# The matrices loaded behind one 512 KB load instead of two, and a slot of input released ahead of VectorE's copies

## The chip, the cores and the metric

One core of a Trainium2 chip. The metric is the device time of one execution in microseconds; lower is better. A core has TensorE (PE: matrix products, from SBUF into PSUM), VectorE (DVE), ScalarE (ACT), GpSimd (POOL) and SyncE (SP), each with an instruction stream of its own, and sixteen DMA engines between HBM and SBUF. The engines order their work by semaphores.

## The reference

```python
# x: (128, 128, 1024) f32; subjects: (128,) int32 in 0..7; weights: (8, 128, 128) f32
w = weights[subjects]
out = jnp.einsum('bct,bcd->bdt', x, w)
return x + out
```

For each of 128 batch entries a 128 x 128 matrix is chosen out of eight by an index, its transpose is multiplied with the entry's 128 x 1024 block, and the block is added. 67 MB are read and 67 MB written.

## The kernel before

The residual is taken into the product: the identity is added to the chosen matrix, so that one product gives x + out. VectorE builds these matrices at run time from the index: `place_rows` (lines 207 to 216) adds `eye` to `w_nat`, the matrices as loaded, and `place` (195 to 205) adds `same` to `w_all`, the matrices in another order of rows.

The batch is worked in 32 tiles of four entries (2 MB in, 2 MB out each). `x_in` has four slots, `x_out` eight. The two sets of PSUM banks, `ps[0]` and `ps[1]`, hold two entries each.

The first four tiles are loaded entry by entry (`load_rows`, 163 to 170: 512 KB each, so sixteen loads), with one row of the entry to a partition; all four slots are filled at the start without any wait. The matrices (512 KB, in rows of 512 B) come between the second and the third of these loads (lines 300 to 307). Sorting matmuls (355 to 363) then bring the matrices into the row order of the later tiles, in `ps[1]`; ACT and VectorE each copy half of that into `w_all` (`sort`). The later 28 tiles are loaded in two transfers of 1 MB (`load`, 151 to 161).

All loads are issued by ACT, all stores by SP, each in program order. A slot of `x_in` may be filled anew when its tile has been multiplied. VectorE says so with `s_eaten`, and ACT waits for it ahead of each load (lines 368 and 374). In the long loop ACT first does its own copies of a tile (`take`), then waits for `s_eaten`, then issues the two loads of the tile four places on.

VectorE's work for one tile: wait for a free output slot (`s_room`), wait for a product (`s_product`), copy it from PSUM to `x_out`, twice, then build the matrices of the tile two places on with four small products (`place_rows` or `place`). `signal` (416 to 419) hangs the tile's signals on these products: the first tells SP that the copies are done (`s_added`), the second releases the input slot (`s_eaten`), the last tells TensorE that the matrices are there (`s_go`). In the first four tiles VectorE makes both copies (`copy_rows`, whole bank sets); in the later ones it copies `ps[0]` in two halves, and ACT copies `ps[1]` with a swap of partition halves.

TensorE multiplies a tile when its matrices (`s_go`) and its input (`s_ready`, passed on by POOL from the loads' semaphores) are there and the banks are free (`s_free`). POOL waits in order for stores (`s_out`, which gives `s_room`) and loads (`s_in`, which gives `s_ready`).

Of the kernel before, what the change touches and what calls it, by code (L numbers as in the profile page):

```python
# [30 lines left out]
H = 2  # L31

P = 2
# [18 lines left out]
FIRST = 4  # L52
# [5 lines left out]
def transfer(nc, engine, out, in_):  # L58

    later, nc._always_lower_symbolic_ap = nc._always_lower_symbolic_ap, False
    ins, outs = engine.lower_ap_dma(in_), engine.lower_ap_dma(out)
    nc._always_lower_symbolic_ap = later
    return engine.add_instruction(
        mybir.InstDMACopy(
            name=nc.get_next_instruction_name(),
            engine=engine.engine,
            ins=ins,
            outs=outs,  # L70
            mode="Copy",
            cce_op=ALU.bypass,
            queue=QUEUES[engine.engine],
        )
    )
# [3 lines left out]
def kernel(  # L79
# [7 lines left out]
    nc = tc.nc  # L87
# [3 lines left out]
    Q = P * H  # L91
# [12 lines left out]
    if room:  # L104
# [26 lines left out]
    s_eye = tc.alloc_semaphore("s_eye")  # L131
# [4 lines left out]
    s_eaten = tc.alloc_semaphore("s_eaten")  # L136
    s_product, s_added, s_free, s_room = (
        [tc.alloc_semaphore(f"s_{name}{p}") for p in range(P)]
        for name in ("product", "added", "free", "room")
    )  # L140
# [22 lines left out]
    def load_rows(i, q):  # L163
        at = (i % IN * Q + q) * T
        transfer(
            nc,
            nc.scalar,
            x_in[:, at : at + T],
            x[i * Q + q].rearrange("(b r) t -> b (r t)", r=C // 32),
        ).then_inc(s_in[i % IN], DMA)  # L170
# [14 lines left out]
    def subjects_of(at):  # L185
        _, subject = nc.values_load_multi_w_load_instructions(
            index[0:1, at],
            engines=[mybir.EngineType.DVE],
            min_val=0,
            max_val=S - 1,  # L190
            skip_runtime_bounds_check_because="the index is clamped on the chip above",
        )
        return subject

    def place(u, subject):
        return [
            nc.vector.tensor_tensor(  # L197
                ws[u][p][h * A : (h + 1) * A],
                w_all[h * A : (h + 1) * A, bass.ds(subject[p * H + h], 1), :],
                same[h * A : (h + 1) * A],  # L200
                ALU.add,
            )
            for p in range(P)
            for h in range(H)
        ]

    def place_rows(u, subject):
        return [
            nc.vector.tensor_tensor(  # L209
                ws[u][q // H][:, :, q % H * D : (q % H + 1) * D],  # L210
                w_nat[:, bass.ds(subject[q], 1), :],
                eye,
                ALU.add,
            )
            for q in range(Q)
        ]
# [42 lines left out]
    def half_of(slot, half):  # L259
        at = slot * (P * SIZE) + half * T  # L260
        banks = slice(half * (T // N), (half + 1) * (T // N))
        return at, banks

    def copy(slot, half):
        at, banks = half_of(slot, half)
        return nc.vector.tensor_copy(  # L266
            x_out[:, bass.ds(at, T)], ps[0][:, banks].rearrange("d b n -> d (b n)")
        )

    def copy_rows(i, p):  # L270
        at = i % OUT * P * SIZE + p * SIZE
        return nc.vector.tensor_copy(  # L272
            x_out[:, at : at + SIZE], ps[p].rearrange("d b n -> d (b n)")
        )
# [22 lines left out]

    with tc.tile_critical():  # L298

        for q in range(H):  # L300
            load_rows(0, q)
        transfer(
            nc,
            nc.scalar,
# [42 lines left out]
        for p in range(P):  # L347
            nc.gpsimd.wait_ge(s_same, H).then_inc(s_room[p], OUT - p * FIRST)

        for q in range(H, FIRST * Q):  # L350
            load_rows(q // Q, q % Q)

        nc.tensor.wait_ge(s_pick, 1)
# [51 lines left out]
        placed = place_rows(0, subject[:Q])  # L405
# [5 lines left out]
        placed = place_rows(1, subject[Q:])  # L411
# [3 lines left out]

        def signal(placed):
            placed[0].then_inc(s_added[0], 1)
            placed[1].then_inc(s_eaten, 1)
            placed[-1].then_inc(s_go, 1)

        for i in range(FIRST):
            subject = subjects_of(slice((i + 2) * Q, (i + 3) * Q))
            nc.vector.wait_ge(s_room[0], 1).then_inc(s_room[0], -1)
            for p in range(P):
                nc.vector.wait_ge(s_product[p], 1).then_inc(s_product[p], -1)  # L425
                copy_rows(i, p).then_inc(s_free[p], 1 if i < FIRST - 1 else R * (1 + p))
            signal((place_rows if i + 2 < FIRST else place)(i % 2, subject))
        with nc.vector.Fori(0, (NT - FIRST) // 2) as turn:  # L428
            for u in range(2):
                subject = subjects_of(bass.ds(turn * (2 * Q) + (u + FIRST + 2) * Q, Q))  # L430
                slot = (turn * 2 + (u + FIRST)) % OUT
                nc.vector.wait_ge(s_room[0], 1).then_inc(s_room[0], -1)
                for half in range(2):
                    nc.vector.wait_ge(s_product[0], H).then_inc(s_product[0], -H)  # L434
                    copied = copy(slot, half).then_inc(s_free[0], 1)
                signal(place(u, subject))
        with nc.tensor.Fori(0, FIRST // 2) as turn:
            for u in range(2):
# [44 lines left out]
```

## Time and profile before

| | before |
|---|---|
| median of 3 runs, us | 328.47 (328.0 to 329.03) |
| profiled execution: its own time, us | 328.55 |
| profiled execution: span, us | 326.8 |
| PE / DVE / ACT / POOL busy | 77% / 44% / 37% / 1% |
| HBM read and written, MB | 67.63 and 67.11 |
| mean over the span, GB/s | 412 |

The span runs from the first to the last event of one execution as the hardware profiler saw it. A page of the profile gives busy time by engine, the span in 40 slices of 8.17 us, queues, and groups of instructions. ACTq and SPq are the instructions with which ACT and SP issue transfers; the transfers run later, on the DMA engines. "L65 DMA_DIRECT2D" is the line of the helper `transfer` that every load and store goes through. In a timeline, a row has its start, its length (of all instructions merged into it), engine, line, operation, output and input; in brackets stands the idle time ahead of it and what ended it. The rows on which the prediction rests stand there.

### The profile page before, as it was taken

How to read it: one execution, taken by the hardware profiler on the slowest of the kernel's cores; microseconds unless marked ns; L12 is line 12 of the kernel's file. 1: busy time of each engine (PE TensorE's matmuls, PEld its weight loads, DVE VectorE, ACT ScalarE, POOL GpSimd, SP SyncE). 2: the span in 40 equal slices, each digit the busy share in tenths (PEclk: the TensorE clock that was granted, in tenths of full speed). 3: DMA queues.
4: the chain of work that ended last, by engine and by line, in shares of the span. 5: the costliest groups of instructions: out<-in, count | busy, mean ns of one | idle time of the engine just before them, and what ended most of it. 6: DMA issues, size and time to landing. Idle time of an engine off the chain costs nothing. (4 is left out here: it accounts for less than half of the span.)

```text
span 326.8 us, 5288 instructions
## 1 busy us (share of the span) xinstructions
PE 251.4 (77%) x1870; PEld 93.5 (29%) x1870; DVE 143.4 (44%) x207; ACT 120.3 (37%) x142; POOL 1.8 (1%) x8
## 2 busy tenths in 40 slices
PE   6899968888888888887495886958886827999300
PEld 2344423333333333333131332313332302333100
DVE  1377855555555555555504455044555050555500
ACT  0200005555555555555504555045555050555500
POOL 2000000000000000000000000000000000000000
PEclk9799999999999999999978999789999776999955
DMA  6999999999999999999999999999999999999990
GB/s 238 424 415 311 434 423 433 428 419 441 423 435 429 429 431 427 435 427 429 427 439 427 419 450 441 425 417 415 453 419 439 437 413 429 449 429 409 441 445 40
DMA packets 8247, 134.81 MB, mean 413 GB/s; under 512 B 1585, under 2 KB 2610, under 8 KB 2610
## 3 DMA queue, kind: packets, MB, share of 16 engines
q10 hardware_dynamic: 4496, 67.64, 49.1%
q1 hardware_dynamic: 3746, 67.11, 48.3%
q8 instruction: 2, 0.03, 0.0%
q14 instruction: 3, 0.02, 0.0%
HBM read 67.63 MB, written 67.11 MB: 412 GB/s over the span
## 5 line engine op out<-in xcount | busy, mean ns | idle before, releaser
L249 PE MATMUL ps<-x_in,w 64*64 64x512 f32 x1792 | 213.5, 619 | 49.6 <-PEq L240 47.5
L278 ACT COPY x_out<-ps 64x1024 f32 (+1 forms) x112 | 112.6, 1006 | 173.5 <-ACTq L293 167.5
L266 DVE COPY x_out<-ps 128x1024 f32 x56 | 68.6, 1224 | 143.6 <-DVEq L434 143.6
L249 PEld LDWEIGHTS ps<-x_in,w 64*64 64x64 f32 x1792 | 77.5, 138 | 185.5 <-issue 185.5
L197 DVE TENSOR_TENSOR w<-w_all,same 64x256 f32<-64x256 f32 x120 | 50.4, 420 | 3.2
L225 PE MATMUL ps<-x_in,w 128*128 x64 | 27.6, 592 | 0.0
L272 DVE COPY x_out<-ps 128x2048 f32<-128x2048 f32 x8 | 18.3, 2291 | 6.0 <-DVEq L425 6.0
L225 PEld LDWEIGHTS ps<-x_in,w 128*128 128x128 f32 x64 | 12.2, 190 | 15.3 <-issue 15.3
L357 PE MATMUL ps<-x_out 128*128 128x512 f32 x8 | 5.4, 836 | 2.3 <-DMA x_out<-in_L_cond_weights_dram 2.3
L313 PE MATMUL ps<-x_out 128*128 128x512 f32 x6 | 5.1, 1028 | 1.7 <-DVE x_out L310 1.7
L209 DVE TENSOR_TENSOR w<-x_out 128x128 f32<-128x128 f32 x16 | 3.6, 285 | 6.1 <-DMA x_out<-in_L_cond_weights_dram 5.9
L284 ACT ACT_TABLE_LOAD x1 | 1.3, 1283 | 12.9 <-issue 12.9
L296 ACT COPY mark<-same 1x1 f32 (+1 forms) x28 | 5.3, 190 | 0.7
L357 PEld LDWEIGHTS ps<-x_out 128*128 128x128 f32 x8 | 2.0, 263 | 6.0 <-issue 6.0
L284 DVE COPY w_all<-ps 128x1024 f32<-128x1024 f32 x1 | 1.2, 1225 | 4.4 <-PE ps L357 4.4
L313 PEld LDWEIGHTS ps<-x_out 128*128 128x128 f32 x6 | 1.8, 328 | 3.7 <-issue 2.1
L284 ACT COPY w_all<-ps 128x1024 f32<-128x1024 f32 x1 | 1.0, 1012 | 0.3 <-PE ps L357 0.3
L310 DVE MEMSET x_out<- 128x512 f32 x1 | 0.5, 485 | 1.0 <-SPq L298 1.0
L381 DVE TENSOR_SCALAR x_out<-x_out 1x128 int32<-1x128 int32 x1 | 0.4, 395 | 0.6 <-DMA x_out<-in_itok_B_dram 0.6
L338 POOL TENSOR_SCALAR_AFFINE_SELECT same<-same 128x256 f32<-128x256 f32 x1 | 0.5, 526 | 0.1
L326 POOL TENSOR_SCALAR_AFFINE_SELECT x_out<-x_out 128x256 f32<-128x256 f32 x1 | 0.4, 423 | 0.0
L338 POOL TENSOR_SCALAR_AFFINE_SELECT same<-x_out 128x256 f32<-128x256 f32 x1 | 0.4, 417 | 0.0
(9 smaller groups left out, 1.4 us busy)
## 6 DMA issues: line engine op xcount, KB each, us to landing
x_in<-in_x_dram ACTq DMA_DIRECT2D x56, 1024.0 KB, 14.3
out_dram<-x_out SPq DMA_DIRECT2D x20, 2048.0 KB, 57.3
out_dram<-x_out SPq DMA_DIRECT2D x6, 4096.0 KB, 45.7
x_in<-in_x_dram ACTq DMA_DIRECT2D x16, 512.0 KB, 9.4
x_out<-in_L_cond_weights_dram ACTq DMA_DIRECT2D x1, 512.0 KB, 6.8
x_out<-in_itok_B_dram SPq DMA_DIRECT2D x1, 0.5 KB
```

Source lines behind the costliest of these rows:

```text
L197: nc.vector.tensor_tensor(ws[u][p][h * A : (h + 1) * A], w_all[h * A : (h + 1) * A, bass.ds(subject[p * H + h], 1), :], same[h * A : (h + ...
L209: nc.vector.tensor_tensor(ws[u][q // H][:, :, q % H * D : (q % H + 1) * D], w_nat[:, bass.ds(subject[q], 1), :], eye, ALU.add,)
L225: mm = nc.tensor.matmul(ps[p][:, bank], ws[u][p][:, 0, h * D : (h + 1) * D], x_in[:, bass.ds(slot * (Q * T) + ((p * H + h) * T + t), N)], ...
L249: mm = nc.tensor.matmul(ps[p][cols, bank], ws[i % 2][p][rows, 0, r * D + e * A : r * D + (e + 1) * A], x_in[rows, at : at + N], start=r == ...
L266: return nc.vector.tensor_copy(x_out[:, bass.ds(at, T)], ps[0][:, banks].rearrange("d b n -> d (b n)"))
L272: return nc.vector.tensor_copy(x_out[:, at : at + SIZE], ps[p].rearrange("d b n -> d (b n)"))
L278: return nc.scalar.copy(x_out[h * A : (h + 1) * A, bass.ds(at + SIZE, T)], ps[1][(1 - h) * A : (2 - h) * A, banks].rearrange("d b n -> d ( ...
L284: engine(w_all.rearrange("c s (r e a) -> c r s e a", r=R, e=R)[:, r], ps[1][:, r * R : (r + 1) * R].rearrange("c g (s a e) -> c (g s) e a" ...
L296: nc.scalar.copy(mark[:, bass.ds(slot, 1)], same[:1, 0, :1]).then_inc(s_added[1], 1)
L313: nc.tensor.matmul(ps[P - 1][:, BANKS - 1], zeros[:, :D], zeros, start=True, stop=True)
L338: nc.gpsimd.affine_select(same[:, 0, :], same[:, 0, :] if h else zeros[:, : R * D], [[2 * C, R], [-2 * C, R], [-1, A]], ALU.not_equal, 1.0 ...
L357: nc.tensor.matmul(ps[1][:, r * R + g], pick[:, r], w_raw[:, g * N : (g + 1) * N], start=True, stop=True,).then_inc(s_picked, 1)
```

## The change

The matrices are issued behind one load of 512 KB instead of two; the second load of tile 0 moves behind them, the order of the rest stays. And the signal `s_eaten` leaves `signal`: VectorE gives it by an instruction of its own, which stands right behind its wait for the tile's last product and ahead of the copy of that product. The instruction waits for `s_eye`, a semaphore that was set at the start and is never taken back, so that it does not hold anything up.

```diff
-        for q in range(H):
-            load_rows(0, q)
+        load_rows(0, 0)
         transfer(
             nc,
             nc.scalar,
...
-        for q in range(H, FIRST * Q):
+        for q in range(1, FIRST * Q):
             load_rows(q // Q, q % Q)
...
         def signal(placed):
             placed[0].then_inc(s_added[0], 1)
-            placed[1].then_inc(s_eaten, 1)
             placed[-1].then_inc(s_go, 1)
+
+        def eaten():
+            nc.vector.wait_ge(s_eye, 1).then_inc(s_eaten, 1)
...
                 nc.vector.wait_ge(s_product[p], 1).then_inc(s_product[p], -1)
+                if p == P - 1:
+                    eaten()
                 copy_rows(i, p).then_inc(s_free[p], 1 if i < FIRST - 1 else R * (1 + p))
...
                     nc.vector.wait_ge(s_product[0], H).then_inc(s_product[0], -H)
-                    copied = copy(slot, half).then_inc(s_free[0], 1)
+                    if half:
+                        eaten()
+                    copy(slot, half).then_inc(s_free[0], 1)
```

On ACT, at the very start of the program, the order of the transfers changes (`in_L_cond_weights_dram` is the matrices, `in_x_dram` the input; a line number is that of the kernel concerned, and moves by what is added or taken above it):

```order
-L479 UNCONDITIONAL_BRANCH x2
-L65 DMA x_in<-in_x_dram 128x1024 x2
+L484 UNCONDITIONAL_BRANCH x2
+L65 DMA x_in<-in_x_dram 128x1024
 L65 DMA x_out<-in_L_cond_weights_dram 128x8x128
-L65 DMA x_in<-in_x_dram 128x1024 x14
+L65 DMA x_in<-in_x_dram 128x1024 x15
 L284 ACT_TABLE_LOAD
 L284 COPY w_all<-ps 128x8x128
```

The matrices stand second instead of third; the sixteen loads stay sixteen.

On VectorE, in each of the first four tiles, with the semaphores that a row waits for (those of the semaphore instructions ahead of it are shown with it):

```order
 L186 TENSOR_LOAD index [waits s_same]
 L272 COPY x_out<-ps 128x2048 [waits s_room0,s_product0]
-L272 COPY x_out<-ps 128x2048 [waits s_product1]
+L272 COPY x_out<-ps 128x2048 [waits s_product1,s_eye]
 L209 ISA
 L209 TENSOR_TENSOR w<-x_out 128x128
```

The release stands between the wait for `s_product1` and the second copy; before, it hung on the second of the products that follow in the last row.

## The prediction, made before the changed kernel was run

> **What bounds the kernel now.** I read the page's slices first, then the stretches of the transfers, then the start instruction by instruction.
>
> ```profile
> PE 251.4 (77%) x1870; PEld 93.5 (29%) x1870; DVE 143.4 (44%) x207; ACT 120.3 (37%) x142; POOL 1.8 (1%) x8
> DMA  6999999999999999999999999999999999999990
> GB/s 238 424 415 311 434 423 433 428 419 441 423 435 429 429 431 427 435 427 429 427 439 427 419 450 441 425 417 415 453 419 439 437 413 429 449 429 409 441 445 40
> HBM read 67.63 MB, written 67.11 MB: 412 GB/s over the span
> ```
>
> No engine is full; the DMA row is, in every slice but the first and the last. The rate stays near 430 GB/s except in slice 0 (238), slice 3 (311, the time from 24.5 to 32.7 us) and the last. So the kernel is bound by the bytes: 134.74 MB at 430 GB/s are 313.3 us, and what a change can win lies in the places where the transfers run below 430. The stretches around them (busy time of each engine, then granted clock, DMA share and GB/s):
>
> ```profile
> 0.00:2.00 2.00, 0.33 (x1) 0.33 (x2) 0.51 (x3) 0.00 (x0) 0.36 (x5) 1.00 0.00 0
> 2.00:5.00 3.00, 3.00 (x4) 1.18 (x4) 1.01 (x3) 0.00 (x0) 1.42 (x4) 1.00 0.98 339
> 5.00:9.00 4.00, 1.80 (x3) 0.34 (x1) 0.00 (x0) 0.00 (x0) 0.00 (x0) 1.00 0.88 307
> 9.00:24.00 15.00, 14.90 (x31) 6.59 (x32) 7.83 (x13) 2.29 (x2) 0.00 (x0) 0.89 1.02 431
> 24.00:26.00 2.00, 2.00 (x6) 0.86 (x5) 1.66 (x4) 0.00 (x0) 0.00 (x0) 1.00 0.74 311
> 26.00:33.00 7.00, 7.00 (x18) 3.12 (x17) 5.52 (x7) 0.00 (x0) 0.00 (x0) 1.00 0.99 309
> 33.00:60.00 27.00, 23.36 (x149) 9.05 (x147) 16.57 (x19) 5.77 (x7) 0.00 (x0) 1.00 1.01 429
> 60.00:309.00 249.00, 199.04 (x1664) 72.05 (x1664) 110.26 (x161) 112.21 (x134) 0.00 (x0) 0.95 1.01 431
> 321.10:325.30 4.20, 0.00 (x0) 0.00 (x0) 0.00 (x0) 0.00 (x0) 0.00 (x0) 0.50 0.05 23
> ```
>
> Against 430 GB/s the stretches lose: 2 to 5 us, 3 x (1 - 339/430) = 0.63 us; 5 to 9 us, 4 x (1 - 307/430) = 1.14; 24 to 26 us, 2 x (1 - 311/430) = 0.55; 26 to 33 us, 7 x (1 - 309/430) = 1.97. With 2 us before the first byte, 2.0 + 0.63 + 1.14 + 0.55 + 1.97 + 313.3 = 319.6 us. The span is 326.8: in the last 7 us the share is 0.05 of sixteen engines, so a single late engine sets the end.
>
> The two losses at 24 to 33 us are of different kinds: at 24 to 26 the share is 0.74, engines stand idle; at 26 to 33 the share is 0.99 and the rate 309, they are busy but slow. Why they stand idle, by the timeline of ACT (the loads' queue), SP (the stores') and VectorE:
>
> ```profile
> 0.91 1.18 ACTq L65 DMA_DIRECT2D x_in<-in_x_dram  x2
> 2.12 0.66 ACTq L65 DMA_DIRECT2D x_out<-in_L_cond_weights_dram  x1
> 2.81 10.05 ACTq L65 DMA_DIRECT2D x_in<-in_x_dram  x14
> 12.90 1.28 ACT L284 ACT_TABLE_LOAD   x1 [12.90 <-issue]
> 14.51 1.01 ACT L284 COPY w_all<-ps 128x1024 f32<-128x1024 f32 x1 [0.33 <-PE ps L357]
> 24.29 1.26 ACTq L65 DMA_DIRECT2D x_in<-in_x_dram  x2
> ...
> 24.00 21.39 SPq L65 DMA_DIRECT2D out_dram<-x_out  x4
> ...
> 9.19 0.90 DVE L209 TENSOR_TENSOR w<-x_out 128x128 f32<-128x128 f32 x4 [5.91 <-DMA x_out<-in_L_cond_weights_dram]
> 15.89 0.90 DVE L209 TENSOR_TENSOR w<-x_out 128x128 f32<-128x128 f32 x4 [0.15 <-DVE w_all L284]
> 18.06 2.29 DVE L272 COPY x_out<-ps 128x2048 f32<-128x2048 f32 x1 [1.28 <-DVEq L425]
> 21.48 2.29 DVE L272 COPY x_out<-ps 128x2048 f32<-128x2048 f32 x1 [1.13 <-DVEq L425]
> 23.69 0.89 DVE L209 TENSOR_TENSOR w<-x_out 128x128 f32<-128x128 f32 x4
> ```
>
> Sixteen loads and the matrices, 17 x 0.524 = 8.91 MB, are queued at the start. Up to 24.0 us the stretches moved 1.02 + 1.23 + 6.47 = 8.7 MB, so the queue runs dry at about 24.5. The next load is issued only at 24.29, behind VectorE's two copies and two products of tile 0 (23.69 + 2 x 0.22 = 24.1), and the first store at 24.00. Both need over a microsecond before bytes move (the first load: issued 0.91, no byte before 2), hence the hole.
>
> **The change: the earlier matrices.** They are issued second instead of third: 1.49 instead of 2.12 (half of 1.18 us earlier, 0.6), behind 0.524 MB less, which at 339 GB/s is 1.55 us. So they land between 0.6 and 1.55 us earlier than now; I take 1.2, and TensorE's first use of them moves from 9.10 to about 7.9.
>
> ```profile
> 9.10 5.37 PE L357 MATMUL ps<-x_out 128*128 128x512 f32 x8 [2.30 <-DMA x_out<-in_L_cond_weights_dram]
> 14.30 27.63 PE L225 MATMUL ps<-x_in,w 128*128 x64
> ...
> 11.00:12.00 1.00, 1.00 (x2) 0.34 (x1) 0.00 (x0) 0.00 (x0) 0.00 (x0) 0.50 0.88 377
> ```
>
> The eight sorting matmuls take 5.37 us now, part of it at a granted clock of 0.50; at full clock one takes 27.63 / 64 = 0.43, eight 3.45. They end between 11.4 and 13.3 instead of 14.30; tile 0's five transfers, 2.62 MB, are in by about 10 as now (2.25 MB up to 9.0, the rest at 431 GB/s). That is not all kept: half of tile 0's products wait for the PSUM banks of the sort, which go free after ACT's copy, and ACT stands in its issues until 12.86, then 1.28 of table load and 1.01 of copy: 15.2 against 15.5 now. So tile 0's second half starts between 15.8 (VectorE's first product behind that copy) and 16.8 (13.3 + 3.45), and ends 3.45 later, 19.3 to 20.2, against 14.30 + 16 x 0.43 = 21.2. VectorE's copy of it and the first store move by the same 1 to 1.9 us: the store to about 22.5.
>
> **The earlier release.** It goes from the second product at 24.1 to the moment when VectorE sees tile 0's second half, 21.5 now and 19.8 with the earlier matrices. ACT waits for nothing else there, so the load of tile 4 is issued near 20, some 4.3 us earlier, while 4.5 us of the first loads still lie in the queue. It cannot land sooner for that, but the queue no longer runs dry: the hole at 24 to 26 goes, 0.55 us.
>
> In the long loop the release gains nothing. There ACT itself is last:
>
> ```profile
> 140.14 4.10 ACT L278 COPY x_out<-ps 64x1024 f32 x4 [3.84 <-ACTq L293]
> 144.23 0.48 ACTq L65 DMA_DIRECT2D x_in<-in_x_dram  x1
> ...
> 143.18 1.76 DVE L197 TENSOR_TENSOR w<-w_all,same 64x256 f32<-64x256 f32 x4
> ```
>
> VectorE's second product ends at 143.18 + 0.88 = 144.06, ACT's own copies, ahead of the load on its queue, at 144.24. The new instruction on VectorE waits for a semaphore long set. One such step shows in the chain as
>
> ```profile
> 305.24 0.06 DVEq L266
> ```
>
> so 32 of them cost 1.9 us of an engine that is 44% busy; behind each stands only the second copy, and TensorE's next tile needs ACT's four copies of 4.10 us anyway, so nothing. Without that cover it would be 28 x 0.06 = 1.7 us. What stands behind on SP and POOL are waits for VectorE's and the loads' signals, which come earlier.
>
> **The slow stretch, 26 to 33 us.** No row shows it without the hole ahead of it. From below: if it comes from starting both queues anew after the hole, it goes with it, a gain of 1.97. From above: if it comes from the loads meeting the first stores, it only moves, 0. Nearest row: 33 to 60 us, where stores of the same four first tiles meet loads at 429 GB/s, so the meeting alone does not cost. I take three quarters, 1.5 us.
>
> The Trainium skill, "DMA: Bandwidth & Descriptors", section "Latency and other measured facts", gives 207 GB/s for copies whose rows lie 512 KiB apart. The first four stores write rows of 4 KB whose four heads are 512 KB apart; by that rule the stretch is the stores' own and would stay (the second rival). The row of 33 to 60 us speaks against it as a whole, the one of 26 to 33 for it where stores run nearly alone.
>
> **The opening, 2 to 9 us.** The same 17 transfers in another order. The matrices' small rows keep costing what they cost (1.14 at 5 to 9); I take 0. At best all of that goes, -1.14; at worst the engines are done with the first load 1.55 us earlier while the matrices are issued only 0.6 earlier, and wait 0.9.
>
> **Sum.** -0.55 - 1.5 + 0 = -2.05 against the profiled execution's 328.55, which is 0.08 above the median of 328.47: 326.5.
>
> **Rivals.** *The late engine keeps the end.* One engine still moves bytes from 321.1 to 325.3 us when the others are done. An engine that is behind has no hole at 24 to 26 (it is still on its first loads when the others stop), so it may gain nothing from the filled hole, and the others' gain ends in a longer wait for it. For it: the share of 0.05. Against: the slow stretch has share 0.99, so it costs that engine too. *The stretch stays.* By the pitch of the first stores only the hole goes: 328.55 - 0.55 = 328.0. Both give 327.6 to 329.0, no change.
>
> *Slower: the matrices are drawn before they are ready.* In 5 to 9 us the share is already 0.88. If the engines stand for the matrices' 1024 small rows behind one load, each loses up to 0.9 us, the late one too; with nothing back at 24 to 33 that is 328.55 + 0.9 = 329.5. It decides from a share below about 0.7 in 4 to 8 us. Against it: issue to first byte was about 1.4 us for the first load, and 1.49 + 1.4 = 2.9 is ahead of that load's end.
>
> *The change does nothing to the loads*: a load issued 4 us earlier waits 4 us longer. Then only holes are worth anything, which is how the sum is made; it belongs to the 328.0 above.
>
> **How the numbers follow.** A gain or loss under 0.3% (1 us) cannot be told from no change here. Forecast, a gain of 1 to 3.7 us: 0.60, most likely 326.5. Late engine or lasting stretch, within 0.3%: 0.29. Slower by over 0.3%: 0.11. The low end: 328.55 - 0.55 - 1.97 - 1.14 = 324.9. The high end takes in the no-change rivals and part of the slower one: 329.2.
>
> **What would show it.** Matrices: the sorting matmuls begin at 7.5 to 8.5 instead of 9.10. Release: a load issue at 19.5 to 20.5 instead of 24.29, a store issue near 22.5. Hole: 24 to 26 us at about 430 GB/s instead of 311. Stretch: 26 to 33 us above 400. Opening: 2 to 9 us no lower than (3 x 339 + 4 x 307) / 7 = 321 GB/s. It is wrong if 24 to 33 us reads 430 and the time stands (late engine), if the low rates return later (stretch), or if the opening falls under 300 (matrices).

## The result and the profile after

| | before | after |
|---|---|---|
| median, us | 328.00 (326.53 to 329.26, 17 runs) | 326.43 (325.62 to 328.88, 17 runs) |
| ratio | | 0.9957, 95% interval 0.9940 to 0.9973 |
| profiled execution / its span, us | 328.55 / 326.8 | 328.88 / 327.1 |

The change makes the kernel 0.43% faster, 1.4 us (0.9 to 2.0). The profiled execution of after happens to be the slowest of its 17 runs; a second profile of the same kernel, 326.80 us with a span of 325.0, stands beside it below (experiment e4). The page of after, the two rows of the transfers in 40 slices:

```profile
DMA  7999999999999999999999999999999999999890
GB/s 230 423 429 427 422 441 423 426 437 419 435 439 421 437 435 425 425 445 421 431 421 439 425 420 435 429 431 459 419 425 431 433 417 425 421 437 437 385 393 20
```

Slice 3, 311 GB/s before, is now 427. In return slices 37 and 38, near the end, have fallen to 385 and 393. The stretches of after (granted clock, DMA share and GB/s at a row's end):

```profile
2.00:5.00 3.00, 3.00 (x4) 1.18 (x4) 1.00 (x3) 0.00 (x0) 1.43 (x4) 1.00 0.86 263
5.00:9.00 4.00, 3.71 (x8) 1.39 (x7) 0.90 (x4) 0.00 (x0) 0.00 (x0) 1.00 1.01 356
9.00:24.00 15.00, 14.00 (x33) 5.91 (x32) 9.11 (x12) 2.29 (x2) 0.00 (x0) 1.00 1.01 428
24.00:26.00 2.00, 2.00 (x6) 0.81 (x5) 0.75 (x2) 0.00 (x0) 0.00 (x0) 1.00 1.02 418
26.00:33.00 7.00, 7.00 (x18) 3.17 (x17) 5.33 (x6) 0.00 (x0) 0.00 (x0) 1.00 0.98 419
321.10:325.30 4.20, 0.00 (x0) 0.00 (x0) 0.00 (x0) 0.00 (x0) 0.00 (x0) 0.50 0.05 23
```

The hole at 24 to 26 us is closed (share 1.02 instead of 0.74), and the slow stretch behind it is gone too (419 GB/s instead of 309). The last row has not changed: one engine of sixteen is still at work when the others are done. The start of after, from the timelines of ACT, SP, VectorE and TensorE:

```profile
1.49 0.66 ACTq L65 DMA_DIRECT2D x_out<-in_L_cond_weights_dram  x1
12.08 1.28 ACT L284 ACT_TABLE_LOAD   x1 [12.08 <-issue]
13.38 1.01 ACT L284 COPY w_all<-ps 128x1024 f32<-128x1024 f32 x1
19.10 8.01 ACTq L65 DMA_DIRECT2D x_in<-in_x_dram  x4
...
21.60 32.99 SPq L65 DMA_DIRECT2D out_dram<-x_out  x5
...
14.54 0.90 DVE L209 TENSOR_TENSOR w<-x_out 128x128 f32<-128x128 f32 x4 [2.75 <-ACT w_all L284]
19.08 2.29 DVE L272 COPY x_out<-ps 128x2048 f32<-128x2048 f32 x1 [1.15 <-DVEq L426]
...
6.86 3.67 PE L356 MATMUL ps<-x_out 128*128 128x512 f32 x8 [0.29 <-DMA x_out<-in_L_cond_weights_dram]
11.53 27.99 PE L225 MATMUL ps<-x_in,w 128*128 x64 [1.00 <-PEq L222]
```

The sorting matmuls start at 6.86 instead of 9.10 and take 3.67 instead of 5.37. The load of tile 4 is issued at 19.10, the moment when VectorE starts its second copy (19.08), instead of 24.29; the first store goes at 21.60 instead of 24.00.

### The profile page after: what moved, and what is told of

Its sections match the earlier page's. It is cut to its first block, busy times and chain, and to the rows that moved or that the text cites. A ratio compares the mean times of both kernels' runs of the same rounds, so it can differ in the third digit from the quotient of the medians.

```text
span 327.1 us, 5320 instructions
## 1 busy us (share of the span) xinstructions
PE 250.2 (76%) x1870; PEld 93.7 (29%) x1870; DVE 143.4 (44%) x207; ACT 120.4 (37%) x142; POOL 1.8 (1%) x8
## 2 busy tenths in 40 slices
DMA packets 8247, 134.81 MB, mean 412 GB/s; under 512 B 1585, under 2 KB 2610, under 8 KB 2610
## 5 line engine op out<-in xcount | busy, mean ns | idle before, releaser
L249 PEld LDWEIGHTS ps<-x_in,w 64*64 64x64 f32 x1792 | 78.5, 138 | 186.2 <-issue 186.2
L312 PE MATMUL ps<-x_out 128*128 128x512 f32 x6 | 4.9, 982 | 1.7 <-DVE x_out L309 1.7
L356 PE MATMUL ps<-x_out 128*128 128x512 f32 x8 | 3.7, 601 | 0.3 <-DMA x_out<-in_L_cond_weights_dram 0.3
```

The lines of the kernel that those rows point to most:

```text
L249: mm = nc.tensor.matmul(ps[p][cols, bank], ws[i % 2][p][rows, 0, r * D + e * A : r * D + (e + 1) * A], x_in[rows, at : at + N], start=r == ...
L312: nc.tensor.matmul(ps[P - 1][:, BANKS - 1], zeros[:, :D], zeros, start=True, stop=True)
L356: nc.tensor.matmul(ps[1][:, r * R + g], pick[:, r], w_raw[:, g * N : (g + 1) * N], start=True, stop=True,).then_inc(s_picked, 1)
```

## The experiments

All are compared with the kernel before, run on the same chip beside them. Between the sets of runs the median of the kernel before differs by up to 0.7 us (327.69 to 328.36), so medians of different sets are compared only roughly. The theory: the rates at 24 to 33 us were lost because the queues ran dry. Its rivals: the slow stretch belongs to the first stores, or a late DMA engine sets the end.

**e1: the matrices alone.**

```diff
-        for q in range(H):
-            load_rows(0, q)
+        load_rows(0, 0)
...
-        for q in range(H, FIRST * Q):
+        for q in range(1, FIRST * Q):
```

> Only the matrices move ahead of the second load; the release stays on the second product. Theory (the hole is what costs; whatever brings the load of tile 4 well ahead of 24.5 us, when the first loads end, wins all of it): VectorE's second product of tile 0 comes at 21.7 us (21.29 + 2 x 0.22 in the changed kernel), the load of tile 4 is issued at about 21.9, and 24 to 33 us read 415 to 430 GB/s as with both parts; ratio to before 0.995 to 0.997. Rival (the two gains add up, each part half): the stretch 24 to 33 us stays between 309 and 419 GB/s and the ratio is 0.997 to 0.999.

**e2: the release alone** (`eaten()` as in the change, the matrices third as before).

> Only the release moves ahead of the copies; the matrices stay third. Theory of the hole: the load of tile 4 is issued at 21.5 us (VectorE's second copy began at 21.48 before), three microseconds ahead of the end of the first loads, and 24 to 33 us read 415 to 430 GB/s though stores still start at 24.0; ratio 0.995 to 0.997. Rival (gains add up): 309 to 419 GB/s, ratio 0.997 to 0.999.

The first load issued after the start, and the stretch of 24 to 33 us, of e1, then of e2:

```profile
21.71 8.05 ACTq L65 DMA_DIRECT2D x_in<-in_x_dram  x4
24.00:33.00 9.00, 9.00 (x22) 3.99 (x21) 6.38 (x8) 0.00 (x0) 0.00 (x0) 1.00 1.02 431
```

```profile
21.25 8.01 ACTq L65 DMA_DIRECT2D x_in<-in_x_dram  x4
24.00:33.00 9.00, 9.00 (x22) 3.98 (x22) 7.29 (x9) 0.00 (x0) 0.00 (x0) 1.00 1.02 417
```

Each part by itself issues the load three microseconds ahead of the end of the first loads, and each brings the rate of 24 to 33 us back (431 and 417, before 309; in e2 the part from 26 to 33 us alone reads 393). By the rates the parts do not add up. The ratios are 0.9978 (0.9951 to 1.0006) and 0.9977 (0.9952 to 1.0002). Both lie in the range that the rival had named, and both intervals reach 1: by the times alone, each part can be told neither from no change nor from both together.

**e3: the first four stores in the later stores' layout**, in the kernel before.

```diff
-        if i < FIRST:
+        if i < 0:
             there = out[i * Q : (i + n) * Q].rearrange("g d t -> d g t")
```

> The kernel before, with one change: the first four stores write rows of 8 KB with heads 1 MB apart, as the later ones do, so that the first four tiles land in another order in the output than the reference's. Theory of the hole: the slow stretch stays, 26 to 33 us at 290 to 340 GB/s, time as before (ratio 0.998 to 1.002). Rival (the stretch belongs to the 4 KB rows 512 KB apart): 26 to 33 us read over 400 GB/s, only the hole at 24 to 26 stays, ratio 0.993 to 0.996.

Its sorting matmuls, the next load, and the two stretches:

```profile
9.02 6.53 PE L357 MATMUL ps<-x_out 128*128 128x512 f32 x8 [3.10 <-DMA x_out<-in_L_cond_weights_dram]
25.37 1.26 ACTq L65 DMA_DIRECT2D x_in<-in_x_dram  x2
24.00:26.00 2.00, 2.00 (x6) 0.92 (x5) 1.66 (x6) 0.00 (x0) 0.00 (x0) 1.00 0.26 107
26.00:33.00 7.00, 7.00 (x18) 3.06 (x17) 5.52 (x7) 0.00 (x0) 0.00 (x0) 1.00 1.05 337
```

Stores in a layout that runs at 431 GB/s later on are followed by the same slow stretch, 337 GB/s. And in after, e1 and e2 the first stores keep their rows, and the stretch is gone. So it is not the rows of the first stores; it follows the hole. The hole itself came out larger (107 GB/s), because the sort took 6.53 us instead of 5.37 at the low clock (below) and the load went 1.1 us later. Ratio 1.0025 (0.9995 to 1.0056).

**e4: both parts again**, the changed kernel, for a second profile.

> The changed kernel once more, for a second profile. Theory of the late engine: its last bytes land some 5 to 6 us behind the fifteen others (at 319 us) in this profile too, and the profiled execution's time follows it. Rival (that late engine belonged to one execution): the last engine is done within 3 us of the others and the profiled execution takes about 326.4 us. Ratio to before 0.995 to 0.997 by both.

The end of the kernel before, of after, and of e4 as the transfers show it between 316 and 327 us, in 40 slices of 0.275 us:

```profile
DMA  9022920299022800200020000200020000000000
```

```profile
DMA  0982299820000200020002000020002000000000
```

```profile
DMA  0209520292000020002000020000000000000000
```

A 2 that stands alone is one packet: a single engine takes one every 1.2 us when the fifteen others are done. From 319.6, 318.2 and 318.5 us on they come singly, and the last one starts at 324.0, 324.3 and 322.3 us. So the late engine is there each time, about 4 to 6 us behind, and the time of the execution follows it: 328.55, 328.88 and 326.80 us. The ratio of e4 is 0.9969 (0.9944 to 0.9994).

Ahead of the last store, by the stretch up to it, of before and of e4, each with the issue of that store:

```profile
307.00:309.50 2.50, 0.00 (x0) 0.00 (x0) 1.28 (x4) 0.71 (x2) 0.00 (x0) 1.00 0.98 419
308.65 0.54 SPq L65 DMA_DIRECT2D out_dram<-x_out  x1
```

```profile
307.00:309.00 2.00, 0.00 (x0) 0.00 (x0) 1.19 (x3) 0.48 (x2) 0.00 (x0) 0.51 0.20 82
308.50 0.54 SPq L65 DMA_DIRECT2D out_dram<-x_out  x1
```

Here most of the gain of the fifteen went. Before, they were busy until the last store (0.98). In e4 the share from 307 to 309 us is 0.20: they have run out of work and stand idle, 2 x (1 - 0.20) = 1.6 us, for a last store that is issued only 0.15 us earlier.

**e6: POOL lets TensorE start ahead of its wait for the output slot.**

```diff
+            landed = DMA * (Q + P * (i // IN))
+            nc.gpsimd.wait_ge(s_in[i % IN], landed).then_inc(s_ready, 1)
             if i - OUT in stored:
                 n, count = stored[i - OUT]
                 for p in range(P):
                     nc.gpsimd.wait_ge(s_out[i % OUT], count).then_inc(s_room[p], n)
-            landed = DMA * (Q + P * (i // IN))
-            nc.gpsimd.wait_ge(s_in[i % IN], landed).then_inc(s_ready, 1)
```

> The changed kernel, with POOL's two waits for a tile in the other order: the loads' (which lets TensorE start) ahead of the stores' (which frees the output slot). Now tile 28's products wait until 271 us for a store that the late engine finishes at 269.6. Theory (the late engine sets the end by its own work): tile 28 is multiplied some 7 us sooner, the last store is issued earlier, the fifteen engines are done earlier, and the end stays: ratio to before 0.994 to 0.998 as with the change alone. Rival (the end follows the last store, which follows the last four tiles): the end moves by 3 us or more with the last store, ratio 0.984 to 0.989.

Tile 28 on TensorE and the last store, in e4 and in e6, and the transfers of e6 between 316 and 327 us:

```profile
271.00 9.71 PE L249 MATMUL ps<-x_in,w 64*64 64x512 f32 x64 [7.29 <-PEq L240]
...
308.50 0.54 SPq L65 DMA_DIRECT2D out_dram<-x_out  x1
```

```profile
260.36 7.45 PE L249 MATMUL ps<-x_in,w 64*64 64x512 f32 x64 [2.65 <-PEq L240]
...
304.69 0.54 SPq L65 DMA_DIRECT2D out_dram<-x_out  x1
...
DMA  9890222020002000020002000000000000000000
```

Tile 28 is multiplied 10.6 us sooner, and the last store goes 3.8 us sooner. The last single packet starts at 321.8 us, only 0.5 us sooner than in e4, and the time hardly moves: median 326.09 against 326.43 and 326.48 of the changed kernel. The ratio is 0.9926 (0.9895 to 0.9958); e7, which is compared with the same runs of the kernel before, has 0.9932. The last store does not set the end; the rival (at most 0.989) is out. It is the lowest median of the study, but it cannot be told from the changed kernel.

**e7: the matrices ahead of all loads.**

> The changed kernel, with the matrices ahead of all loads instead of behind one. Theory (earlier matrices are worth only the hole, and that is closed): the sorting matmuls start about 1.2 us earlier than in the changed kernel if TensorE is free (it is busy with its idle products until 6.6, so at 6.6), 24 to 33 us stay at 415 to 430 GB/s, ratio to before 0.994 to 0.998, the same as with the change. Rival (the start of the chain itself is worth time): another 0.5 to 1.2 us, ratio 0.991 to 0.994.

The sorting matmuls:

```profile
6.95 3.65 PE L355 MATMUL ps<-x_out 128*128 128x512 f32 x8
```

They start at 6.95 us as in e4, without an idle time ahead of them: until then TensorE is at its idle products. The median, 326.47, is that of the change (326.43 and 326.48). The ratio, 0.9932 (0.9901 to 0.9964), lies in the rival's range, and its interval covers the theory's too; e6, which starts as the change does, has 0.9926 against the same runs. So no gain on the change is seen, but a small one is not excluded. The rate of 24 to 33 us is 408 GB/s, a little under what was expected.

**e5: the last store over fifteen engines.**

```diff
-    def store(i, n):
+    def store(i, n, rows=slice(None)):
...
-            there,
-            x_out[:, at : at + n * P * SIZE].rearrange("a (o f) -> a o f", o=1),
+            there[rows],
+            x_out[rows, at : at + n * P * SIZE].rearrange("a (o f) -> a o f", o=1),
...
-    last = store(*stores[-1])
...
+    for rows in (slice(0, 120), slice(120, C)):
+        last = store(*stores[-1], rows)
...
```

> The changed kernel, with the last store (4 MB) cut in two: 120 partitions, which the transfer can only spread over fifteen DMA engines, and the 8 others. One engine, if it is the last of the sixteen, so has up to 9.75 us less to move (319.6 - 309.9 in the kernel before, from its start to the end of the fifteen), the others 0.65 us more (9.75 x 128/120), eight of them a row of 1.2 us besides. Theory (one engine that is behind sets the end, and it is always this one): the end falls to that of the others, 320.5 to 321.5 us, ratio to before 0.984 to 0.990. Rival a (it is another engine, or one that changes): the end is 0.6 to 1.9 us later than with the change, ratio 0.998 to 1.003. Rival b (the late engine is only what the profile shows, not what bounds the timed runs): ratio within 0.998 to 1.003 too, with the tail gone in the profile.

```profile
309.00:320.00 11.00, 0.00 (x0) 0.00 (x0) 0.00 (x0) 0.00 (x0) 0.00 (x0) 0.50 0.90 241
```

A miss: ratio 1.0207 (1.0127 to 1.0287). In this row of its stretches the engines are busy (0.90) and move 241 GB/s, where e4 has 384. This store of 120 partitions is slow in itself, so the run tells nothing about the late engine.

**e8 to e11: extra work for some of the engines.**

```diff
+            if i == NT - 4:
+                nc.sync.wait_ge(s_spare, 8 * DMA)
             store(i, n).then_inc(s_out[i % OUT], DMA)
+            if i == 8:
+                there = out.rearrange("b (a r) t -> (b a) (r t)", r=R)[(NT - 1) * Q * A :]
+                for j in range(8):
+                    rows = slice(j * 8, (j + 1) * 8)
+                    transfer(
+                        nc, nc.sync, there[rows], w_all[rows].rearrange("c s d -> c (s d)")
+                    ).then_inc(s_spare, DMA)
```

> The changed kernel, with eight extra stores of 8 partitions each behind the ninth store (8 rows of 8 KB from w_all, into rows of the last tile that are written over later). A transfer of 8 rows can be spread over eight DMA engines at most, so eight engines have 64 KB more each, 2 x 1.22 = 2.4 us. Theory (one engine, always the same, is 4 to 6 us behind and sets the end; the others have that much in hand): the end moves by 2.4 us if that engine is among the eight (ratio to before about 1.003), and by nothing if it is not (about 0.996, as with the change alone). Rival (all engines bound the time, through the stores that every tile waits for): 8/16 of it, 1.2 us, ratio 0.9995.

> The same with 12 rows in each extra store, twelve engines at most. Theory: 2.4 us if the late engine is among the twelve (ratio about 1.003), nothing if not (0.996). Rival: 12/16 of it, 1.8 us, ratio 1.001.

> The same with 15 rows, fifteen engines at most. Theory: 2.4 us unless the late engine is the one left out (ratio 1.003, or 0.996). Rival: 15/16 of it, 2.3 us, ratio 1.003.

> The same with 16 rows, all sixteen engines: 1 MB more in all, 2.4 us. Both: the end moves by 2.4 us against the change alone, ratio to before about 1.003. If it does not, the extra work lies in time in which the late engine stands idle, and the reading of the other three falls.

The packets of the kernel before and of e8:

```profile
DMA packets 8247, 134.81 MB, mean 413 GB/s; under 512 B 1585, under 2 KB 2610, under 8 KB 2610
DMA packets 8375, 135.33 MB, mean 414 GB/s; under 512 B 1649, under 2 KB 2674, under 8 KB 2674
```

The eight extra stores bring 128 packets: 64 of 8 KB with the rows, and 64 under 512 B (1649 instead of 1585), eight for each store, which fits a store that is cut in eight parts.

| rows in an extra store | median, us | ratio to before | over the change's 326.45 |
|---|---|---|---|
| 8 | 328.98 | 1.0045 (1.0012 to 1.0079) | 2.5 |
| 12 | 329.11 | 1.0035 (1.0010 to 1.0059) | 2.7 |
| 15 | 329.14 | 1.0053 (1.0027 to 1.0079) | 2.7 |
| 16 | 329.97 | 1.0078 (1.0051 to 1.0105) | 3.5 |

The last column compares different sets of runs; from the ratios and the change's 0.9957 it would be 2.9, 2.6, 3.1 and 4.0 us. Either way, half of the engines with 2.4 us more already cost the whole 2.4 us; a share of 1.2 us would have been 0.9995, outside the interval. That does not yet single out one engine: any engine held up by 2.4 us might cost as much. That the sixteenth engine costs another 0.8 us was not foreseen and stays open.

**e12: stairs.** The same place, with two stores each of 1, 2, ... 8 rows.

> The changed kernel, with the extra stores as stairs: two each of 1, 2, ... 8 rows of 8 KB. A store of k rows goes to the first k engines, so the first engine gets sixteen rows more (16 x 0.31 = 4.9 us), the next fourteen, and so on to the eighth with two (0.6 us). Theory (one engine among the first eight is 4 to 6 us behind; the others have that much in hand): the end moves by that engine's own extra alone, 0.6 us for the eighth, 1.2 for the seventh, up to 4.9 for the first: ratio to before 0.998 for the eighth, 1.001 for the sixth, 1.007 for the third, 1.011 for the first. Anything well under 4.9 us shows that engines with more extra work than that had it in hand. Rival (any engine that is held up by so much sets the end): 4.9 us, ratio 1.011.

Median 329.11, ratio 1.0021 (0.9998 to 1.0044), 2.7 us more than the change (2.1 by the ratios). If the rows fall on the engines as expected, an engine with 4.9 us of extra work does not delay the end by 4.9 us, so engines are there that have time in hand, and that rival (1.011) is out. By the stairs and the interval the late engine would be about the fourth to the seventh, but e11 shows that the extra stores cost something besides, so which one it is stays open. No row of the profile numbers the engines. That a transfer of k rows goes to the lowest-numbered k engines is what the Trainium skill states ("DMA: Bandwidth & Descriptors", section "Why a DMA increments its semaphore by 16 and not by 1"); the sizes of the effects do not speak against it, and nothing here shows it directly. So the stairs argue for one late engine; they do not show it.

## Why the prediction was right, and where its size was off

**The earlier matrices:** the first use came at 6.86 instead of 7.5 to 8.5, 2.2 us earlier than before and so beyond the bound of 1.55 us that the prediction gave; why is not shown. The sort then ran at full clock and was over at 10.5. Tile 0's second half waited for ACT's copy, as said, but ACT's issues ended at 12.06 and not at 12.86 as in the kernel before, so the copy began at 13.38, VectorE's products behind it at 14.54 instead of 15.8, and the second half was seen at 19.08 instead of 19.3 to 20.2. All of this only feeds the hole, as said; e7 shows no gain from more of it.

**The release:** right, with the load at 19.10 (said 19.5 to 20.5) and the store at 21.60 (said 22.5), each a little earlier, as the second half was. That it gains nothing in the long loop was not tried by itself; the rate of 60 to 309 us, 431 GB/s before and 430 in e2, shows no gain there.

**The hole, 0.55 us, and the slow stretch, 1.5 of 1.97 us:** both went, the stretch more than the three quarters taken: at 24 to 33 us after and e4 read 419 and 430 GB/s against 309, which is 9 x 110 / 430 = 2.3 us and 2.5 us. e1 and e2 show that either way to an early load does it; e1, e2 and e3 refute the rival of the first stores' rows. In these stores only the four heads of one partition lie 512 KB apart; the rows of neighbouring partitions lie 4 KB apart. Nor do stores run nearly alone in the stretch, as the prediction read it: 1.11 MB of stores and 1.05 MB of loads start in it. Why the engines run slow for 7 us after a hole is not shown; the trace shows that each packet takes longer (a 16 KB packet of the stores 0.80 us on average, in the next 7 us 0.61; a 32 KB packet of the loads 1.77, then 1.21).

**The opening, 0:** (3 x 263 + 4 x 356) / 7 = 316 GB/s against 321, 0.1 us lost. Right.

**The sum, 2.05 us:** measured 1.4, interval 0.9 to 2.0. By the rates the regained time was, if anything, larger, 2.3 us. The step that was too large is the one that puts it to the end in full. The fifteen others gave 1.6 us back as a wait for the last store (e4), and when that wait is taken away (e6) the end stays: it is that of the late engine, which was only a rival in the prediction.

That rival was right about who ends last, but not in its reason, that an engine already behind at 24 us has no hole to fill. The traces keep the moment at which each of the sixteen parts of a store or load reports to its semaphore. Before, the last part of the first loads reports 0.1 us behind the fifteenth. The second and the third store are complete at 53.4 and 65.6 us before, and each is 1.8 us earlier in after (1.8 and 1.9 in e4). So the engine that was last there took part in the gain, with 1.8 of the 2.3 us. In after and e4 the last part of a store comes at most 1.2 us behind the fifteenth up to 175 us, and 1.6 to 6.7 us behind it from 184 us on (before: 4.0 us in the first store, 1.5 at 175 us, then 1.2 to 5.7). The late end of the changed kernel thus arises long behind the hole; why is not known.

The predicted time of 326.5 was met at 326.43, partly by luck: the forecast was made from 328.55, and 17 runs put the kernel before at 328.0, which hides part of the error.

**The slower rival:** the engines' share at 2 to 5 us fell from 0.98 to 0.86, so they did wait a little for the matrices, but at 5 to 9 it rose from 0.88 to 1.01. Together that is the 0.1 us of the opening.

## What to carry to other kernels

Where the transfers bound the time, look in the slices for the places in which they run below their steady rate, and behind a hole also for the slow stretch that follows it: here the hole was 0.55 us and what came with it 1.97. One early signal is enough; parts that close the same hole do not add up. Then see who ends last: what all engines gain on average is not what the last one gains.

## What was not expected of the hardware

One of the sixteen DMA engines ends 4 to 6 us behind the others in the profiles of before, after and e4 (by the last and the fifteenth part of the last store; 2.8 to 4.8 us in e1 to e3, e6 and e7), though the packets of the stores and the later loads are all of 16 or 32 KB; why is not known. The profile also counts five packets of the kind "instruction": two of 16 KB, about 1 us each, and three of 8 KB, 0.31 us each, all ahead of 193 us. Which engines carried them is not shown.

The idle gap ahead of the sort sets TensorE's clock. The stretch of 9 to 14 us, of before, of e3 and of after:

```profile
9.00:14.00 5.00, 4.90 (x8) 2.15 (x9) 0.90 (x4) 1.10 (x1) 0.00 (x0) 0.66 1.03 436
```

```profile
9.00:14.00 5.00, 4.98 (x6) 2.15 (x7) 0.90 (x4) 1.28 (x1) 0.00 (x0) 0.50 1.00 423
```

```profile
9.00:14.00 5.00, 4.00 (x10) 1.63 (x9) 1.23 (x1) 1.91 (x2) 0.00 (x0) 1.00 0.98 416
```

After 2.30 us without work (before) the granted clock is 0.66 on average and the sort takes 5.37 us, after 3.10 us (e3) 0.50 and 6.53, after 0.29 us (after) 1.00 and 3.67. The Trainium skill ("TensorE: Matmul & The Clock Gate", section "Part 1: The HAM clock gate") says that the clock is halved after an idle window of about 3.4 us and that the windows run freely; here 2.30 us of idle time were enough for it. That this phase is also what spreads the times of the kernel before (326.04 to 330.46 in 34 of the 35 runs beside e1 to e4, the changed one 326.02 to 328.31 in 12) was not tried, and e1, which has the short gap, spreads from 326.01 to 329.60.

A store of 120 partitions ran at 241 GB/s with a share of 0.90 (e5); its 32 KB packets took 1.9 us on average instead of 1.22.
